# The product of theta and phi by seven products of 128 by 128

## The chip, the cores and the metric

The kernel runs on one core of a Trainium2 chip. The metric is the device time of one execution in microseconds (us); lower is better. All numbers are fp32.

## The reference

The input is `x`, 8 images of 512 channels and 32 by 32 positions (n = 1024). The first layer is an attention block with 8 heads and a residual. The second is a nonlocal block followed by a normalization over the batch. The change lies in the second layer:

```python
theta_x = _conv1x1(x, theta_w, theta_b).reshape(b, C_INTER, n)      # C_INTER = 256
phi_x = _conv1x1(x, phi_w, phi_b).reshape(b, C_INTER, n)
f_div_C = jnp.einsum('bcn,bdn->bcd', theta_x, phi_x) / n            # 256 by 256, a sum over 1024 positions
y = jnp.einsum('bcd,bdn->bcn', f_div_C, g_x).reshape(b, C_INTER, h, w)
z = _conv1x1(y, W_w, W_b) + x
```

## The kernel before, in words

The program is one straight line of instructions for 8 images, with buffers and waits set by a tile framework. The function `unshifted` does the work. A second function, `shifted`, is there for inputs whose scores would be too large, and is not entered in the runs shown.

For each image `b` the loop at L816 runs: attention (`attention`, scores at L462, weighted sums at L488); queries, values and keys of the next image (`heads_of`, `values`); the projection (`project`); theta and phi together (`theta_phi`, L610); and the nonlocal part (`nonlocal_`, L640).

Most large products are already made by the seven-product scheme, which replaces the eight products of a 2 by 2 block product by seven, with extra sums of blocks. `seven` (L263) writes the matmuls at L300, product after product (numbered 0 to 6). After each product it calls `read`, which adds the result into SBUF, and then a function given in `between` for that number. So `between` is how work of other kinds is put among the products.

Theta times phi is not made in that way. `make_f` (L630) makes it as 2 by 8 matmuls: for each half of theta's 256 columns, eight blocks of 128 positions are summed in PSUM, each by a 128 by 128 weight (theta) against 256 columns (theta's block of positions of `phi`). In this program's fp32, every matmul is recorded as two matmul records, each with a weight load of its own. The result `f`, 128 by 512 elements in one PSUM bank, goes to SBUF by one ScalarE instruction, which also applies the factor 1/n (L637). It is written into a spare part of the tile that holds the weights of `g`.

`nonlocal_` runs the seven products of `g` (called `pg`), and calls `make_f` after product 5 (L662). Then `f` and the weights `ww` give the folded weights `wf` (L670, two products of two matmuls, `pwf`; ScalarE copies them to SBUF at L671). From `wf` and `g` come the last seven products (`pz`), preceded by sums of `g` (L683, tiles `tg`) and sums of `wf` (L686, tile `ws`) on VectorE.

The tile `tp` holds theta in columns 0 to 255 and phi in columns 256 to 511, in eight blocks of 128 positions. It is complete in steps: theta's two halves after products 5 and 3 of `ptp`, phi's two halves after products 4 and 6.

What sets the order: instructions wrapped in `pe`, `dve` or `sp` stay in the written order on their engine; the framework places the others by its own estimates. Blocks such as `ww`, `wf` and the sums come from a ring of ten buffers (`block`, L76), handed out in turn: a new block waits until the buffer's last readers are done. Weights come by `load_w` (L124) from two buffers in turn, through the DMA queue of SyncE (SP); so a weight load waits until the product that used the buffer is over, and what is behind it in the queue waits too. `ww` is loaded through the same queue (L643).

Images 0 to 4 go through `pz` at once. Image 5 stops after `wf`, which is put aside with `g` for the end (`late`). Image 6's `f` is made inside the attention of image 7, and image 7 is the last.

Of the kernel before, what the change touches and what calls it, by code (L numbers as in the profile page):

```python
# [11 lines left out]
ALU = mybir.AluOpType  # L12
# [4 lines left out]
P = 128  # L17
# [13 lines left out]
def unshifted(ctx: ExitStack, tc: tile.TileContext, a: dict, out: bass.AP):  # L31
    nc = tc.nc
    B, C, H, W = a["x"].shape
    N = H * W
    CC = C // P
    NB = N // P
# [4 lines left out]
    CI = a["WgT"].shape[1]  # L41
    IC = CI // P
# [19 lines left out]
    def pe(ins):  # L62
        tc.keep_in_program_order(ins)

    dve = sp = pe
# [10 lines left out]
    def block(name):  # L76
        return ring.tile([P, 2, 512], F32, tag="e", name=name)
# [14 lines left out]
    theta, phi = (a[n].rearrange("(c p) f -> p c f", p=P) for n in ("WthetaT", "WphiT"))  # L92
# [10 lines left out]
    def weight_sums(w, a21, which=(3, 4, 5, 6), pin=lambda ins: None):  # L103
        for to, l, r, op in ((3, a21, w[:, 2], ALU.add), (4, w[:, 3], w[:, 0], ALU.subtract),
                             (5, w[:, 0], a21, ALU.subtract), (6, w[:, 1], w[:, 4], ALU.subtract)):
            if to in which:
                pin(nc.vector.tensor_tensor(w[:, to], l, r, op))
# [9 lines left out]
    rest = {}  # L117
# [24 lines left out]
    def weights(name, sums_done=False):  # L142

        n, w = loaded.pop(0)
        assert n == name
        if name not in kept:
            if not sums_done:
                weight_sums(w, corner[name])
            if name not in ("WqT", "WkT"):
                keep("plain" if name == "WpT" else name, w)  # L150
        return w

    def keep(name, w):
        kept[name] = dram.tile([P, 14 * w.shape[3]], F32, tag=f"kept_{name}", name=f"kept_{name}")
        nc.sync.dma_start(kept[name], w.rearrange("p i k f -> p (i k f)"))
# [172 lines left out]
    xt = xp.tile([P, CC, N], F32, tag="x", name="x_0")  # L328
    heads = const.tile([P, P], F32, tag="heads", name="heads")
    nc.vector.memset(heads, 0.0)  # L330
    _, w_first = weights_tile("WqT", C // 2)
    loaded.append((queue.pop(0), w_first))
    corner["WqT"] = block("a21_WqT")[:, :, :C // 2]
    for x_part, w_part in (((0, 1, 0), (w_first[:, 0], 0, 0, 0, 1)), ((1, 2, 0), (w_first[:, 0], 0, 0, 1, 2)),
                           ((2, 4, 0), (w_first[:, 1], 0, 1, 0, 2)), ((0, 1, 1), (w_first[:, 2], 1, 1, 0, 2)),
                           ((1, 2, 1), (corner["WqT"], 1, 0, 0, 2)), ((2, 4, 1), ())):
        c0, c1, h = x_part
        at = slice(h * 512, (h + 1) * 512)
        nc.sync.dma_start(xt[:, c0:c1, at], x_v[0, :, c0:c1, at])
        if w_part:  # L340
            to, m, k, c0, c1 = w_part
            nc.scalar.dma_start(to[:, c0:c1], quarter("WqT", m, k)[:, c0:c1])
    ps = next_bank("warm_ps")[:, 0, :]
# [263 lines left out]
              early=b == B - 1, inner="WpT" if 0 < b < B - 1 else None)  # L607


    def theta_phi(b, w, data, between):  # L610
        tp = mats.tile([P, NB, 2 * CI], F32, tag="o", name=f"tp_{b}")

        def at(q):
            return tp[:, (int(q[1]) - 1) * NB // 2:int(q[1]) * NB // 2, (int(q[0]) - 1) * CI:int(q[0]) * CI]

        def as_tp(ps):
            return ps.rearrange("p h (i f) -> p (h i) f", f=CI)

        def first(q, ps):
            ins = nc.vector.tensor_tensor(at(q), as_tp(ps), tpb[:, int(q[0]) - 1].to_broadcast([P, NB // 2, CI]),  # L620
                                          ALU.add)
            if q == "11":
                dve(ins)

        seven(f"ptp_{b}", w, data, True, first,
              lambda q, ps: nc.vector.tensor_tensor(at(q), at(q), as_tp(ps), ALU.add),
              {0: lambda: "t3" in data or more_sums(data, (3, 4), pin=dve), **between})
        return tp

    def make_f(b, tp, ps):  # L630
        f = rest["WgT"][:, :IC * CI].rearrange("p (c d) -> p c d", c=IC)
        ps = ps[:, 0, :].rearrange("p (c d) -> p c d", c=IC)
        for c in range(IC):
            for i in range(NB):
                pe(nc.tensor.matmul(ps[:, c, :], tp[:, i, c * P:(c + 1) * P], tp[:, i, CI:],  # L635
                                    start=(i == 0), stop=(i == NB - 1)))
        nc.scalar.mul(f, ps, 1.0 / N)  # L637
        return f

    def nonlocal_(b, xt, data, f, wg, before_wf, between=None):  # L640

        ww = block(f"ww_{b}")
        nc.sync.dma_start(ww, a["WwT"].rearrange("(c p) f -> p c f", p=P))  # L643
        g = [w3.tile([P, N], F32, tag="acc", name=f"g_{b}_{d}") for d in range(IC)]
        fs = [f]

        def f_meanwhile():
            fs[0] = f(next_bank(f"pf_{b}"))

        def part(q):  # L650
            return g[int(q[0]) - 1][:, cols(q)]

        def first(q, ps):
            d = int(q[0]) - 1
            if between and q == "21":
                nc.vector.tensor_scalar(part(q), ps[:, 0, :], gb[:, d:d + 1], 1.0, ALU.add, ALU.mult)
            else:
                nc.scalar.activation(part(q), ps[:, 0, :], AF.Identity, bias=gb[:, d:d + 1])  # L658

        seven(f"pg_{b}", wg, data, False, first,  # L660
              lambda q, ps: nc.vector.tensor_tensor(part(q), part(q), ps[:, 0, :], ALU.add),
              between or {5: f_meanwhile}, early=bool(between))  # L662
        f = fs[0]

        before_wf()
        wf = block(f"wf_{b}")
        for d in range(IC):
            ps = next_bank(f"pwf_{b}_{d}")[:, 0, :]
            for c in range(IC):
                pe(nc.tensor.matmul(ps, f[:, c, d * P:(d + 1) * P], ww[:, c, :], start=(c == 0), stop=(c == IC - 1)))  # L670
            nc.scalar.copy(wf[:, d, :], ps)  # L671
        if b >= B - LATE:
            late[b] = xt, g, wf
            return
        half = C // 2
        ws = block(f"ws_{b}")
        w = [wf[:, 0, :half], wf[:, 1, :half], wf[:, 1, half:]] + [ws[:, i, j * half:(j + 1) * half]
                                                                 for i in range(2) for j in range(2)]
        tg = block(f"tg0_{b}"), block(f"tg1_{b}")
        t = [tg[i // 2][:, i % 2, :] for i in range(4)]  # L680
        b11, b12, b21, b22 = (g[k][:, h * 512:(h + 1) * 512] for k in range(2) for h in range(NH))
        for to, l, r in ((t[0], b12, b11), (t[1], b22, t[0]), (t[2], b22, b12), (t[3], b21, t[1])):
            nc.vector.tensor_tensor(to, l, r, ALU.subtract)  # L683
        for to, l, r, op in ((3, wf[:, 0, half:], w[2], ALU.add), (4, w[3], w[0], ALU.subtract),
                             (5, w[0], wf[:, 0, half:], ALU.subtract), (6, w[1], w[4], ALU.subtract)):
            nc.vector.tensor_tensor(w[to], l, r, op)  # L686

        class Blocks:
            shape = (P, 7, 1, half)

            def __getitem__(self, at):
                _, i, k, m = at
                return w[i][:, m]

        def first_z(q, ps):
            for m in range(2):
                c = rows(q).start + m
                at = xt[:, c, cols(q)]
                nc.vector.scalar_tensor_tensor(at, ps[:, m, :], wb[:, c:c + 1], at, ALU.add, ALU.add)

        data = {"11": b11, "21": b21, "22": b22, "t1": t[0], "t2": t[1], "t3": t[2], "t4": t[3]}
        data = {n: d.rearrange("p (k n) -> p k n", k=1) for n, d in data.items()}
        seven(f"pz_{b}", Blocks(), data, False, first_z, add_to(xt))
        for oc in range(CC):
            for h in range(NH):
                nc.vector.bn_stats(stats[:, oc, b * NH + h, :], xt[:, oc, h * 512:(h + 1) * 512])
            nc.sync.dma_start(spill[b][:, oc, :], xt[:, oc, :])
# [83 lines left out]
    b11, b12, b21, b22 = quarters_of(xt)  # L791
    t = [block(f"t{i}_x_0") for i in range(4)]
# [7 lines left out]
    data = {"11": b11, "21": b21, "22": b22, "t1": t[0], "t2": t[1], "t3": t[2], "t4": t[3]}  # L800
# [15 lines left out]
    for b in range(B):  # L816
# [22 lines left out]
        between = None  # L839
        if not last:  # L840
# [25 lines left out]
            later_k = []  # L866
# [5 lines left out]
        else:  # L872
# [3 lines left out]
            between = {4: late_unit(b - 1, 0, sums_now=False)}  # L876
# [14 lines left out]
        data = data_sums(quarters_of(xt), f"x1_{b}", (1, 2, 3, 4) if last else (1, 2))  # L891
        if last:
            reload_chunks(B - LATE)
        elif b > B - LATE and b != B - 2:
            z[b] = [xt[:, cc, :] for cc in range(CC)]
        tp = theta_phi(b, weights("tp"), data, {} if last else
                       {1: lambda: [one() for one in later_k[:2]], 2: lambda: [one() for one in later_k[2:]],
                        4: lambda: bound_scores(b + 1, q, k, peak_q, peak_k)})
        load_w(nc.sync)

# [9 lines left out]
        if b == B - 2:  # L910
            held.update(x=xt, tp=tp)
        else:
            nonlocal_(b, xt, data, lambda ps: make_f(b, tp, ps), weights("WgT"), before_wf)
            load_w(nc.sync)
            if b in spill_g:
                put_away(b)
        xt = nxt.get("x")
# [6 lines left out]
    ps = next_bank("count")[:, 0, :]  # L924
# [214 lines left out]
```

## Time and profile before

| | |
|---|---|
| median of 4 runs | 2149.22 us (2148.83 to 2150.01) |
| the profiled execution, as timed | 2149.39 us |
| its span in the profile | 2147.6 us |
| TensorE matmuls (PE) | 2124.4 us busy |
| weight loads (PEld) | 1123.0 us busy, beside the matmuls |
| VectorE (DVE) | 1401.8 us busy |
| ScalarE (ACT) | 746.1 us busy |
| GpSimd (POOL) | 193.2 us busy |

The time of the execution is 1.8 us more than its span. PE and PEld are one engine with two rows: a weight load can run while an earlier matmul streams. A matmul's recorded length holds its latency, so that the pace of a row of matmuls is read from the distance of their starts. In a line of the timeline the first two numbers are the start and the length of a merged group in us, "x32" is its number of records, and the bracket is the engine's idle time before it and what ended that. `pf` is the PSUM tile of theta times phi, and `w_WgT` in `w_WgT<-pf` is the tile that holds `f`.

### The profile page before, as it was taken

What the parts mean: (1) busy time and instruction counts of PE and PEld (TensorE: products, weight loads), DVE (VectorE), ACT (ScalarE), POOL (GpSimd) and SP (SyncE); (2) the same over time, 40 slices, a digit from 0 to 9 for tenths busy, and PEclk for the clock granted to TensorE, in tenths of its full rate; (3) what the DMA queues carried; (4) which work ended last, traced back from release to release, by engine and by line L of the source; (5) the groups of instructions that cost most, each with busy time, mean ns of one, the idle gap of its engine ahead of it and who ended that gap; (6) DMA issues with size and microseconds to landing.
All of it is one profiled execution on the core that took longest, in us unless ns stands there. A gap on an engine that the chain in (4) does not pass through costs nothing.

```text
span 2147.6 us, 30080 instructions
## 1 busy us (share of the span) xinstructions
PE 2124.4 (99%) x12510; PEld 1123.0 (52%) x12510; DVE 1401.8 (65%) x1699; ACT 746.1 (35%) x854; POOL 193.2 (9%) x242
## 2 busy tenths in 40 slices
PE   9999999999999999999999999999999999999996
PEld 4534664356733567335663366633666347743462
DVE  6466666667576675766657667576674676757736
ACT  1464104641046310463105621056212652056106
POOL 0111000110001100011000100011000110001000
PEclk9999999999999999999999999999999999999998
DMA  6433443334143331433324343233434235122758
GB/s 241 137 46 62 135 163 126 50 72 127 73 130 48 80 116 72 133 50 81 110 98 113 48 100 98 98 107 50 107 139 151 40 48 139 52 60 38 225 200 340
DMA packets 53967, 231.02 MB, mean 108 GB/s; under 512 B 9792, under 2 KB 16192, under 8 KB 46272
## 3 DMA queue, kind: packets, MB, share of 16 engines
q1 hardware_dynamic: 42144, 199.26, 27.5%
q0 software_dynamic: 10192, 28.46, 11.0%
q8 instruction: 100, 1.64, 0.3%
q10 hardware_dynamic: 1488, 1.32, 0.2%
q14 instruction: 43, 0.35, 0.1%
HBM read 141.84 MB, written 46.27 MB: 88 GB/s over the span
## 4 chain that ended last, share of the span: by engine, by line
PE 97%; ACT 1%; DVE 1%; DMA 0%; issue 0%; SPq 0%; DVEq 0%; ACTq 0%
PE ps L462 21%; PE po L488 20%; PE pv L300 9%; PE ptp L300 9%; PE pp L300 7%; PE pq L300 6%; PE pk L300 6%; PE pg L300 4%; PE pk_in_s L255 3%; PE pq_in_s L255 3%; PE pf L635 3%; PE pz L300 2%; PE pp_in_s L255 2%; PE pwf L670 1%; ACT z L787 1%; PE pz L746 1%
## 5 line engine op out<-in xcount | busy, mean ns | idle before, releaser
L465 ACT ACTIVATE e<-ps 128x1024 f32<-128x1024 f32 x512 | 522.5, 1024 | 431.3 <-PE ps L462 425.8
L471 DVE TENSOR_TENSOR acc<-acc,e 128x1024 f32<-128x1024 f32 x384 | 469.9, 1224 | 143.6 <-ACT e L465 140.3
L462 PE MATMUL ps<-q,k 64*64 64x512 f32 x4096 | 529.4, 590 | 0.0
L488 PE MATMUL po<-e,v 64*64 64x512 f32 x4096 | 528.7, 589 | 0.0
L488 PEld LDWEIGHTS po<-e,v 64*64 64x64 f32 x4096 | 156.6, 133 | 282.8 <-issue 275.4
L462 PEld LDWEIGHTS ps<-q,k 64*64 64x64 f32 x4096 | 155.5, 133 | 283.8 <-issue 274.8
L501 POOL DMA_DIRECT2D fold<-acc x189 | 147.2, 779 | 982.3 <-DMA fold<-acc 573.7
L469 DVE TENSOR_TENSOR acc<-e,e 128x1024 f32<-128x1024 f32 x64 | 78.3, 1224 | 144.0 <-ACT e L465 144.0
L658 ACT ACTIVATE g<-pg,gb 128x512 f32<-128x512 f32 x31 | 21.3, 687 | 407.6 <-PE pg L300 407.5
L300 PE MATMUL pv<-w_WvT,t_x 128*128 128x256 f32 x512 | 116.4, 381 | 0.0
L300 PE MATMUL ptp<-w_tp,t_x 128*128 128x256 f32 x512 | 114.4, 379 | 0.0
L417 ACT COPY v<-pv 128x1024 f32<-128x1024 f32 x32 | 32.4, 1012 | 213.9 <-PE pv L300 213.9
L300 PEld LDWEIGHTS pv<-w_WvT,t_x 128*128 128x128 f32 x512 | 96.6, 190 | 18.5 <-issue 5.7
L300 PEld LDWEIGHTS ptp<-w_tp,t_x 128*128 128x128 f32 x512 | 97.3, 190 | 13.2
L300 PE MATMUL pp<-t_o,w_WpT 128*128 128x512 f32 x208 | 100.8, 592 | 0.0
L300 PE MATMUL pk<-t_x,w_WkT 128*128 128x512 f32 x200 | 100.0, 592 | 0.0
L300 PE MATMUL pq<-t_x,w_WqT 128*128 128x512 f32 x200 | 99.8, 592 | 0.0
L429 POOL TENSOR_SCALAR q<-q,gates 128x1024 f32<-128x1024 f32 x32 | 35.1, 1108 | 718.8 <-DVE gates L427 718.8
L300 PE MATMUL ptp<-w_tp,x 128*128 128x256 f32 x384 | 87.4, 381 | 0.0
L300 PE MATMUL pv<-w_WvT,x 128*128 128x256 f32 x384 | 86.8, 379 | 0.0
L324 DVE TENSOR_TENSOR q<-q,pq_in_s 128x256 f32<-128x256 f32 x119 | 48.5, 419 | 51.2 <-PE pq_in_s L255 38.5
L324 DVE TENSOR_TENSOR k<-k,pk_in_s 128x256 f32<-128x256 f32 x119 | 47.8, 418 | 50.0 <-PE pk_in_s L255 36.1
(178 smaller groups left out, 2297.6 us busy)
## 6 DMA issues: line engine op xcount, KB each, us to landing
fold<-acc POOLq DMA_DIRECT2D x189, 128.0 KB, 3.1
w_WqT<-kept_WqT SPq DMA_DIRECT2D x7, 2368.0 KB, 8.8
w_WkT<-kept_WkT SPq DMA_DIRECT2D x7, 2368.0 KB, 9.0
r<-den_d SPq DMA_DIRECT2D x32, 512.0 KB, 7.4
x<-in_x_dram SPq DMA_DIRECT2D x30, 512.0 KB, 5.7
w_WpT<-kept_WpT SPq DMA_DIRECT2D x6, 2176.0 KB, 8.4
w_WvT<-kept_WvT SPq DMA_DIRECT2D x7, 1792.0 KB, 7.1
w_tp<-kept_tp SPq DMA_DIRECT2D x7, 1792.0 KB, 7.2
```

Source lines behind the costliest of these rows:

```text
L255: pe(nc.tensor.matmul(ps, a[wi], d[di], start=s not in begun, stop=True, skip_group_check=True))
L300: pe(nc.tensor.matmul(to_ps, lhsT(k), rhs(k), start=(s, at) not in begun, stop=(k == nk - 1), skip_group_check=True))
L324: pin(nc.vector.tensor_tensor(at, at, ps if len(ps.shape) == 3 else ps.unsqueeze(1), ALU.add))
L417: seven(f"pv_{b}", w, data, True, lambda q, ps: nc.scalar.copy(at(q), as_v(ps)), lambda q, ps: dve(nc.vector.tensor_tensor(at(q), at(q), a ...
L429: nc.gpsimd.tensor_scalar(q[:, p, :], q[:, p, :], gate[:, p:p + 1], 1.0, ALU.mult, ALU.mult)
L462: pe(nc.tensor.matmul(ps[c * P // 2:(c + 1) * P // 2, j, :], k[r, p, keys], q[r, p, h * 512:(h + 1) * 512], start=True, stop=True, skip_gr ...
L465: nc.scalar.activation(e, ps, AF.Exp, scale=SCALE)
L469: nc.vector.tensor_tensor(accs[u], es[u, 0], e, ALU.add)
L471: ins = nc.vector.tensor_tensor(accs[u], accs[u], e, ALU.add)
L488: pe(nc.tensor.matmul(ps[j * D:(j + 1) * D, r, :], v[keys, m, (2 * p + j) * D:(2 * p + j + 1) * D], e[keys, j, :], start=(m == 0), stop=(m ...
L501: nc.gpsimd.dma_start(to, part_of, accum_op=ALU.add)
L635: pe(nc.tensor.matmul(ps[:, c, :], tp[:, i, c * P:(c + 1) * P], tp[:, i, CI:], start=(i == 0), stop=(i == NB - 1)))
```

## The change

For images 0 to 5, `f` is made by the seven-product scheme as well. Images 6 and 7 stay with `make_f`.

- `f_sums` (new) makes four sums of 128 by 512 elements of theta on VectorE, and later four of phi. The blocks are halves of the 256 columns and halves of the positions. Theta's sums are called after product 5 of `ptp`, phi's at the start of `nonlocal_`, ahead of the load of `ww`. They take four ring buffers.
- `seven_f` (new) makes seven products of four matmuls each, 128 by 128 weights against 128 columns. They go to seven regions of two PSUM banks. One copy and seven additions on VectorE then make the four blocks of `f`. One of theta's sums is overwritten with an intermediate sum.
- `f` is called after product 4 of `pg`, where it was called after product 5.
- The factor 1/n goes from the ScalarE instruction on `f` (which is gone in these images) to the ScalarE instruction that copies `wf`.

```diff
+    def f_sums(b, tp, k0):
+        name = f"{'phi' if k0 else 'theta'}_{b}"
+        both = block(f"s0_{name}"), block(f"s1_{name}")
+        t = [both[i // 2][:, i % 2, :].rearrange("p (i f) -> p i f", f=P) for i in range(4)]
+        c1, c2 = ([tp[:, h * NB // 2:(h + 1) * NB // 2, k0 + c * P:k0 + (c + 1) * P] for h in range(2)]
+                  for c in range(2))
+        if k0:
+            b11, b21, b12, b22 = *c1, *c2
+            ops = ((0, b12, b11, ALU.subtract), (1, b22, t[0], ALU.subtract), (2, b22, b12, ALU.subtract),
+                   (3, b21, t[1], ALU.subtract))
+        else:
+            b11, b12, b21, b22 = *c1, *c2
+            ops = ((0, b21, b22, ALU.add), (1, t[0], b11, ALU.subtract), (2, b11, b21, ALU.subtract),
+                   (3, b12, t[1], ALU.subtract))
+        for to, l, r, op in ops:
+            dve(nc.vector.tensor_tensor(t[to], l, r, op))
+        return {"11": b11, "12": b12, "21": b21, "22": b22, **{f"s{i + 1}": t[i] for i in range(4)}}
+
+    def seven_f(theta, phi, ps):
+        f = rest["WgT"][:, :IC * CI].rearrange("p (c d) -> p c d", c=IC)
+        at = [ps[:, i // 4, i % 4 * P:(i % 4 + 1) * P] for i in range(7)]
+        for to, l, r in zip(at, ("11", "s2", "12", "s3", "s1", "22", "s4"), ("11", "s2", "21", "s3", "s1", "s4", "22")):
+            for i in range(NB // 2):
+                pe(nc.tensor.matmul(to, theta[l][:, i, :], phi[r][:, i, :], start=(i == 0), stop=(i == NB // 2 - 1),
+                                    skip_group_check=True))
+        f11, f12, f21, f22 = (f[:, c, d * P:(d + 1) * P] for c in range(2) for d in range(2))
+        u = theta["s1"][:, 0, :]
+        dve(nc.vector.tensor_copy(f11, at[0]))
+        for to, l, r, op in ((u, f11, at[1], ALU.add), (f11, f11, at[2], ALU.add), (f22, u, at[3], ALU.add),
+                             (f12, u, at[4], ALU.add), (f21, f22, at[5], ALU.add), (f22, f22, at[4], ALU.add),
+                             (f12, f12, at[6], ALU.add)):
+            dve(nc.vector.tensor_tensor(to, l, r, op))
+        return f
...
+        if theta:
+            phi = f_sums(b, tp, CI)
+            f = lambda ps: seven_f(theta, phi, ps)
         ww = block(f"ww_{b}")
...
-              between or {5: f_meanwhile}, early=bool(between))
+              between or {4 if theta else 5: f_meanwhile}, early=bool(between))
...
-            nc.scalar.copy(wf[:, d, :], ps)
+            nc.scalar.mul(wf[:, d, :], ps, 1.0 if scaled else 1.0 / N)
...
+                       {5: lambda: b < B - 2 and of_theta.append(f_sums(b, tps[0], 0)), 1: lambda: [one() for one in later_k[:2]], 2: lambda: [one() for one in later_k[2:]],
```

More of the change, by code (lines that the diff above doesn't have):

```diff
@@ L607, in project @@
               early=b == B - 1, inner="WpT" if 0 < b < B - 1 else None)
+    tps = []
     def theta_phi(b, w, data, between):
         tp = mats.tile([P, NB, 2 * CI], F32, tag="o", name=f"tp_{b}")
+        tps[:] = [tp]
         def at(q):
@@ L638, in make_f, with nonlocal_ @@
         return f
-    def nonlocal_(b, xt, data, f, wg, before_wf, between=None):
+    def nonlocal_(b, xt, data, f, wg, before_wf, between=None, theta=None, tp=None):
+        scaled = theta is None
+        if theta:
+            phi = f_sums(b, tp, CI)
+            f = lambda ps: seven_f(theta, phi, ps)
         ww = block(f"ww_{b}")
@@ L895, in unshifted @@
             z[b] = [xt[:, cc, :] for cc in range(CC)]
+        of_theta = []
         tp = theta_phi(b, weights("tp"), data, {} if last else
-                       {1: lambda: [one() for one in later_k[:2]], 2: lambda: [one() for one in later_k[2:]],
+                       {5: lambda: b < B - 2 and of_theta.append(f_sums(b, tps[0], 0)), 1: lambda: [one() for one in later_k[:2]], 2: lambda: [one() for one in later_k[2:]],
                         4: lambda: bound_scores(b + 1, q, k, peak_q, peak_k)})
@@ L912, in unshifted @@
         else:
-            nonlocal_(b, xt, data, lambda ps: make_f(b, tp, ps), weights("WgT"), before_wf)
+            nonlocal_(b, xt, data, lambda ps: make_f(b, tp, ps), weights("WgT"), before_wf,
+                      theta=of_theta[0] if of_theta else None, tp=tp)
             load_w(nc.sync)
```

## The prediction

> **What bounds the kernel now.** I read the page's first part, then its chain of work that ended last, then the waits of TensorE. The first fence is part 1 of the page, the second the chain by engine, the third the longest waits of the matmuls (engine and line, what was waited for, total us, times, longest).
>
> ```profile
> PE 2124.4 (99%) x12510; PEld 1123.0 (52%) x12510; DVE 1401.8 (65%) x1699; ACT 746.1 (35%) x854; POOL 193.2 (9%) x242
> ```
>
> ```profile
> PE 97%; ACT 1%; DVE 1%; DMA 0%; issue 0%; SPq 0%; DVEq 0%; ACTq 0%
> ```
>
> ```profile
> PE warm_ps L345 <- DVE heads L330: 1.1, 1, 1.1
> PE den L434 <- PE pg L300: 0.6, 1, 0.6
> ```
>
> TensorE is the chain from end to end and waits for about 2 us in all. So a microsecond taken from its matmul stream comes off the time, as long as nothing else becomes late; VectorE and ScalarE work is free as long as it stays under a matmul. Next, the stage itself, in the timeline of image 2: first TensorE, then VectorE.
>
> ```profile
> 845.12 1.88 PE L300 MATMUL pg<-x,w_WgT 128*128 128x512 f32 x4
> 846.84 7.07 PE L635 MATMUL pf<-tp 128*128 128x256 f32 x32
> 853.75 1.88 PE L300 MATMUL pg<-t_x,w_WgT 128*128 128x512 f32 x4
> 855.47 3.60 PE L670 MATMUL pwf<-ww,w_WgT 128*128 128x512 f32 x8
> 858.90 1.88 PE L300 MATMUL pz<-g,wf 128*128 128x512 f32 x4
> ```
>
> ```profile
> 836.74 1.23 DVE L620 TENSOR_TENSOR tp<-ptp,tpb 128x1024 f32<-128x1024 f32 x1 [2.23 <-PE ptp L300]
> 843.66 0.69 DVE L661 TENSOR_TENSOR g<-g,pg 128x512 f32<-128x512 f32 x1 [5.70 <-PE pg L300]
> ...
> 848.37 0.68 DVE L683 TENSOR_TENSOR tg<-g,g 128x512 f32<-128x512 f32 x1
> 848.98 0.68 DVE L683 TENSOR_TENSOR tg<-g,tg 128x512 f32<-128x512 f32 x1
> 858.00 0.42 DVE L686 TENSOR_TENSOR ws<-wf 128x256 f32<-128x256 f32 x1 [8.34 <-ACT wf L671]
> ```
>
> Theta times phi holds TensorE from 846.84 to 853.75: 6.91 us for 32 records, 0.216 each. Records of 512 columns come at 0.429 (1.72 for four). Both are a little under 0.84 ns a column plus 2 ns: the columns set the pace, not the weight loads. VectorE has two holes in this stage, 5.70 and 8.34 us.
>
> How fast are records of 128 columns? No warm stream of them is in the trace. Two places bound it: the warm-up at the start, which is 16 such records at half the clock (first row), and four products of one column in image 0, where only weight loads of the same size follow each other (two rows, five loads apart).
>
> ```profile
> 1.13 3.49 PEld L345 LDWEIGHTS warm_ps<-heads 128*128 128x128 f32 x16 [1.13 <-DVE heads L330]
> ...
> 218.31 0.19 PEld L191 LDWEIGHTS den<-ones,fold 128*128 128x128 f32 x1
> ...
> 218.87 0.19 PEld L191 LDWEIGHTS den<-ones,fold 128*128 128x128 f32 x1
> ```
>
> Warm-up: the last of 16 loads (333 ns long) starts at 4.29, so one every 0.21 us; halved, about 0.107. That is the pace of the columns alone, with a load for each record beside them. One column: (218.87 - 218.31) / 5 = 0.112 us from load to load.
>
> **What the Trainium skill says.** "TensorE: Matmul & The Clock Gate", section "LDWEIGHTS (loading the stationary operand)", gives a load as its columns over 1.2, 107 ns for 128; the 0.112 above agrees. The same page, "Back-to-back issue gap", says that in streams of loads and matmuls the pace is set by both, with 81 ns for 128 columns where the matmul alone takes 56: 25 ns more than perfect overlap. The rows here show no such loss, but no warm stream of this size either. "PSUM — Partial Sum Buffer", "PSUM bank collisions raise a hardware error", says that engines are to be kept apart by bank, not by address. The order of instructions of the changed kernel agrees: of the eight VectorE instructions that read `pf`, only the first, the copy, waits for TensorE, so it waits for all seven products.
>
> **The change, part by part** (times of image 2; the six images repeat it to 0.01 us).
>
> *Matmuls.* Removed: 32 records, 6.91 us. Added: 7 products x 4 matmuls x 2 records = 56. Columns fall from 32 x 256 = 8192 to 56 x 128 = 7168, weight loads rise from 32 to 56. At the pace of the columns, 0.109 (half of 0.216 plus half of the fixed 2 ns), it is 6.10 us, a gain of 0.80; at the pace of the loads, 0.112, it is 6.27, a gain of 0.64; with the skill's 25 ns added, 0.134 to 0.137, it is 7.5 to 7.7, a loss of 0.6 to 0.8. The change gains as long as a record takes less than 6.91 / 56 = 0.123. I take 0.112: a load starts as the matmul before it starts, and the next matmul cannot start before that load is in, whatever its columns; and in the warm-up both lie fully beside each other. Six images: 6 x 0.64 = 3.8 us.
>
> *Theta's sums.* Four of 128x512 at 0.61 from start to start (the L683 rows: 848.37, 848.98) are 2.4 us. They follow the sum of product 5 (ends 834.5) and fill the 2.23 us hole before 836.74, so phi's last addition starts 0.3 late. Nothing on TensorE waits for it then.
>
> *Phi's sums.* Another 2.4 us, in the 5.70 us hole: from 838.2 to 840.7. The products now start at 845.12, since `pg` product 5 comes after them: 4.4 us to spare.
>
> *The sums of `f`.* They wait for the last product, at 845.12 + 6.27 = 851.39, and start at 851.6. A 128x128 VectorE operation has 0.28 to 0.29 us (L169) and comes each 0.3 us or so. Copy and five sums give f11 and f21 at 853.4. The addition of `pg` product 5 is next on VectorE (it can't run before 853.3), then two sums: done at 854.6. TensorE meanwhile has two products of `pg`, 3.43 us, and reaches `pwf` at 854.8, where f11 and f21 are wanted first; f12 and f22 are wanted at 856.5. To spare: 1.4 and 1.9 us. If the cover were gone, each us of lateness would cost six. Queued behind this wait on VectorE is only the sum of `pg` product 5, then the three `tg` sums, 854.6 to 856.4. Before, they were done at 849.7; they now have 0.9 us until the first `ws` sum, which comes when `wf` does, as before.
>
> *ScalarE.* One 0.60 us instruction less for each image, and the copy of `wf` becomes a multiplication of the same size (0.59 and 0.60): nothing on the path, since between `f` and `pwf` it had 1.7 us of `pg` as cover already.
>
> *DMA order.* On the SP queue `ww` stood ahead of the next `w_WqT`; in the changed kernel it stands behind it, so it is held by that load's wait for the end of `ptp`. The rows are the SP timeline, then the page's median us to landing.
>
> ```profile
> 812.75 0.39 SPq L643 DMA_DIRECT2D ww<-in_WwT_dram  x1
> 836.74 0.33 SPq L134 DMA_DIRECT2D w_WqT<-kept_WqT  x1
> ...
> w_WqT<-kept_WqT SPq DMA_DIRECT2D x7, 2368.0 KB, 8.8
> ...
> ww<-in_WwT_dram SPq DMA_DIRECT2D x8, 512.0 KB, 5.5
> ```
>
> `ww` goes out at 837.1 instead of 812.75. Behind the whole of `w_WqT` and with a fifth more of its time it lands near 836.7 + 8.8 + 2 = 847.5; `pwf` wants it at 854.8. Hidden, with 7 us to spare; uncovered, it would hold TensorE by what is missing. `w_WqT` itself is wanted an attention later. In image 5 the reloads of `x` and the putting aside of `g` change places behind `ww`; both lie in front of an attention of some 110 us (871 to 981). The four ring buffers fall to blocks whose readers are done: the sums take those of the projection's sums, over by 812.
>
> Sum: -3.8 us on TensorE, nothing elsewhere. From the profiled execution's 2149.39 it gives 2145.6; the median shown is 0.17 lower, so 2145.4.
>
> **The rivals.**
>
> *The pace of the columns.* If loads hide wholly, 0.109 a record: 6 x 0.80 = 4.8 us, 2144.4. The warm-up speaks for it; the 0.112 from load to load speaks against.
>
> *Loads and matmuls get in each other's way when warm.* Place: the 56 records of `pf`. At 0.137 each, 7.67 us, 0.76 more than now in each image: +4.6 us, 2153.8, slower. It decides from 0.123 on. For it: the skill's sustained figure, and that loads and columns here need nearly the same time, so that neither has slack. Against: the warm-up, where they also need the same, at exactly the pace of the columns.
>
> *`f` or `ww` comes late at `pwf`.* It takes VectorE steps over 0.5 us (six steps from 851.6 to 854.8), or `ww` over 17 us to land, to begin; 0.64 us of lateness an image eats the gain, and the time stays at 2149.2. Against: the margins above.
>
> **How the numbers follow.** Chances: likeliest case (0.112, all hidden) 0.62; pace of the columns 0.14; loads and matmuls in each other's way 0.15; late `f` or `ww` 0.09. The bound of 0.2% is 4.3 us, about what a measurement of this kernel can tell from no change; the likeliest case, -3.8, lies just inside, and with half a us from the runs and 1 ns on the pace (0.3 us) I give a fifth of it, 0.13, to over 4.3. Faster: 0.13 + 0.14 = 0.27. Slower: 0.13 of the third case and 0.03 of the last = 0.16. Within: 0.57. The range goes from 2143.8 (the column pace, and half a us) to 2150.5 (a pace of 0.127, or a late `f`); past it lie most of the third case and little else.
>
> **What would show it.** Right: the `pf` group is 56 records over about 6.27 us from its first start to the next `pg`, in all six images; no idle time on TensorE before `pwf` and `pz`; the VectorE copy starts after the last product; `ww` issued just after `w_WqT`. Wrong: starts over 0.123 apart, a wait of `pwf` for VectorE or for a DMA, or a wait of the second `pz` product for `ws`.

## The result, and the profile after

| | median, us | runs |
|---|---|---|
| before | 2149.57 (2148.83 to 2153.03) | 52 |
| after | 2145.8 (2144.84 to 2147.97) | 32 |

The ratio of after to before is 0.9982, with a 95% interval of 0.9978 to 0.9987: faster by 0.18%, or 3.8 us. The forecast was 2145.4 us, and a gain of 3.8. That the two agree to a tenth is in part luck: single runs of one kernel lie up to 4.2 us apart, and the stages themselves gained 3.9 us, as shown below.

The span fell from 2147.6 to 2143.4 us. First the three views that said what bounds the kernel, for the kernel after: busy time by engine, the chain by engine, the longest waits of the matmuls.

```profile
PE 2119.6 (99%) x12654; PEld 1123.7 (52%) x12654; DVE 1447.7 (68%) x1795; ACT 743.0 (35%) x848; POOL 193.2 (9%) x242
```

```profile
PE 97%; ACT 1%; DVE 1%; DMA 1%; issue 0%; ACTq 0%
```

```profile
PE warm_ps L345 <- DVE heads L330: 1.1, 1, 1.1
PE pq L300 <- DVE t_x L842: 0.7, 1, 0.7
PE den L434 <- PE pg L300: 0.5, 1, 0.5
```

TensorE is still the chain. VectorE works 46 us more and none of it shows in the waits. There are 144 more matmul records (6 x 24), and yet TensorE is busy for 4.8 us less. The wait of `pq` lies in the start-up of image 0, where the first loads come in.

The stage of image 2 again, TensorE in the timeline after:

```profile
842.12 1.88 PE L300 MATMUL pg<-t_x,w_WgT 128*128 128x512 f32 x4
843.84 1.05 PE L658 MATMUL pf<-tp 128*128 128x128 f32 x8
844.73 1.06 PE L658 MATMUL pf<-s_phi,s_theta 128*128 128x128 f32 x8
845.62 1.06 PE L658 MATMUL pf<-tp 128*128 128x128 f32 x8
846.52 1.95 PE L658 MATMUL pf<-s_phi,s_theta 128*128 128x128 f32 x16
848.30 1.06 PE L658 MATMUL pf<-s_phi,tp 128*128 128x128 f32 x8
849.20 1.06 PE L658 MATMUL pf<-tp,s_theta 128*128 128x128 f32 x8
850.09 1.88 PE L300 MATMUL pg<-x,w_WgT 128*128 128x512 f32 x4
851.81 1.88 PE L300 MATMUL pg<-t_x,w_WgT 128*128 128x512 f32 x4
853.52 3.60 PE L713 MATMUL pwf<-ww,w_WgT 128*128 128x512 f32 x8
```

The group of `pf` goes from 843.84 to 850.09: 6.25 us for 56 records, 0.1116 each, where it was 6.91 for 32; the other five images have the same two lengths to 0.01 us. No bracket with an idle time stands ahead of `pwf` at 853.52. VectorE in the same stage:

```profile
832.00 1.22 DVE L629 TENSOR_TENSOR tp<-tp,ptp 128x1024 f32<-128x1024 f32 x1 [2.38 <-PE ptp L300]
833.26 1.51 DVE L649 TENSOR_TENSOR s_theta<-tp 128x512 f32<-128x512 f32 x1
834.80 0.69 DVE L649 TENSOR_TENSOR s_theta<-s_theta,tp 128x512 f32<-128x512 f32 x1
...
836.61 1.22 DVE L623 TENSOR_TENSOR tp<-ptp,tpb 128x1024 f32<-128x1024 f32 x1
...
850.29 0.29 DVE L662 COPY w_WgT<-pf 128x128 f32<-128x128 f32 x1 [5.56 <-PE pf L658]
850.62 0.29 DVE L666 TENSOR_TENSOR s_theta<-w_WgT,pf 128x128 f32<-128x128 f32 x1
850.94 0.29 DVE L666 TENSOR_TENSOR w_WgT<-w_WgT,pf 128x128 f32<-128x128 f32 x1
851.14 0.48 DVE L666 TENSOR_TENSOR w_WgT<-s_theta,pf 128x128 f32<-128x128 f32 x2
851.54 0.28 DVE L666 TENSOR_TENSOR w_WgT<-w_WgT,pf 128x128 f32<-128x128 f32 x1
852.01 0.69 DVE L704 TENSOR_TENSOR g<-g,pg 128x512 f32<-128x512 f32 x1 [0.19 <-PE pg L300]
```

The copy starts 0.20 us after TensorE has gone on from the last product to `pg` at 850.09, so VectorE did wait for all seven. The copy reads only the first of the two banks, and that one was full after four products; whether it could start then, 2.7 us earlier, no run tries. f11 is in SBUF at 851.23 and f21 at 851.82; `pwf` begins at 853.52. The first sum of theta took 1.51 us and not 0.69, which the prediction did not have; the run `theta_later` below takes that up.

Where in the program the time went is seen from one small product, `bound`, which runs once for each image. Its first and last start enclose all six changed stages. The lines give records, lengths in ns, then the two starts; before, then after:

```profile
L425 PE MATMUL bound<-peak_q,heads x16: 169/210/253, 67.7 to 1871.5; 128*128 128x4 f32 x16
```

```profile
L425 PE MATMUL bound<-peak_q,heads x16: 169/210/253, 67.7 to 1867.6; 128*128 128x4 f32 x16
```

From 1803.8 to 1799.9: 3.9 us, and 6 x (6.907 - 6.251) is 3.9. The other 0.3 us of the two spans lie outside the six stages. Outside them two things differ from execution to execution in all the traces below: the first loads (the first `bound` starts between 67.7 and 69.1), and the last image's reload of its softmax denominators (TensorE stood for it between 0 and 2.2 us). What is left outside differs by some tenths. So in what follows a kernel's effect is read between its first and last `bound`, and the times of single runs are taken with a grain of salt.

### The profile page after: what moved, and what is told of

The parts are those of the page before. It is cut to its first block, busy times and chain, and to the rows that moved or that the text cites. A ratio compares the mean times of both kernels' runs of the same rounds, so it can differ in the third digit from the quotient of the medians.

```text
span 2143.4 us, 30444 instructions
## 1 busy us (share of the span) xinstructions
PE 2119.6 (99%) x12654; PEld 1123.7 (52%) x12654; DVE 1447.7 (68%) x1795; ACT 743.0 (35%) x848; POOL 193.2 (9%) x242
## 4 chain that ended last, share of the span: by engine, by line
PE 97%; ACT 1%; DVE 1%; DMA 1%; issue 0%; ACTq 0%
PE ps L462 21%; PE po L488 21%; PE pv L300 9%; PE ptp L300 9%; PE pp L300 7%; PE pk L300 6%; PE pq L300 5%; PE pg L300 5%; PE pk_in_s L255 3%; PE pq_in_s L255 3%; PE pz L300 2%; PE pf L658 2%; PE pp_in_s L255 2%; PE pwf L713 1%; ACT z L830 1%; PE pz L789 1%
```

## The experiments

Ratios are to the kernel before, on the same chip; "between the bounds" is the distance just explained (before 1803.8, after 1799.9).

### columns_96: what sets the pace of 0.1116

```diff
-                pe(nc.tensor.matmul(to, theta[l][:, i, :], phi[r][:, i, :], ...
+                n = P if i == 0 else 96
+                pe(nc.tensor.matmul(to[:, :n], theta[l][:, i, :], phi[r][:, i, :n], ...
```

> The changed kernel, with columns 96 to 127 left out in three of the four matmuls of each of the seven products. If the weight loads set the pace (my theory), the pf group keeps its 56 records at 0.112 us, 6.25 us from its first start to the next pg, and the time stays near 2145.8. If the columns set it, the 42 narrow records come at 0.082 (96 x 0.84 ns + 2 ns): 14 x 0.112 + 42 x 0.082 = 5.0 us, and the time is 7.5 us lower.

One run, 2146.69 us. The timeline of its `pf`, image 2, first row, last row and what follows:

```profile
844.73 1.03 PE L659 MATMUL pf<-tp 128*128 128x128 f32 x8
...
850.06 1.06 PE L659 MATMUL pf<-tp,s_theta 128*128 128x128 f32 x8
850.95 1.48 PE L300 MATMUL pg<-x,w_WgT 128*128 128x512 f32 x3
```

The group takes 6.22 us, with a quarter of the columns gone from three matmuls in four. (A merged row prints the shape of its first record.) Between the bounds 1799.9, the same as the changed kernel's. The columns do not set the pace at 128 columns; something that the full and the narrow records have in common does: the load of 128 weight columns, or a fixed time.

### columns_96_weights_64: the load, or a fixed time for issuing

```diff
-                pe(nc.tensor.matmul(to, theta[l][:, i, :], phi[r][:, i, :], ...
+                n, m = (P, P) if i == 0 else (96, 64)
+                pe(nc.tensor.matmul(to[:m, :n], theta[l][:, i, :m], phi[r][:, i, :n], ...
```

> As columns_96, and the same three of four matmuls load only 64 of the 128 weight columns, so half of the output partitions are left out of them too. If the time of a load goes with its columns, a load of 64 is over in half of 0.107 and the 96 columns set the pace: 0.082 for the narrow records, 5.0 us for the group, about 7.5 us less in all than the changed kernel. If 0.112 is a fixed time for issuing a load and a matmul, nothing changes: 6.25 us.

One run, 2152.83 us: 1806.7 between the bounds, 6.8 more than the changed kernel, where 7.5 less was expected. The forecast of the total missed, yet the question asked is answered inside the group. Two loads of 64 columns in a run of six narrow records, three loads apart, each from a short stretch of the timeline:

```profile
846.75 0.14 PEld L659 LDWEIGHTS pf<-tp 128*64 128x64 f32 x1
...
846.99 0.14 PEld L659 LDWEIGHTS pf<-tp 128*64 128x64 f32 x1
```

(846.99 - 846.75) / 3 = 0.08: the pace of 96 columns, as forecast. So 0.1116 is not a fixed time for issuing a load and a matmul; with half the weight columns it is gone, while the moving columns are as in `columns_96`. Together the two runs leave the load of 128 weight columns. What was not forecast lies between the narrow and the full records:

```profile
846.30 1.02 PE L659 MATMUL pf<-tp 128*128 128x128 f32 x8
847.25 1.13 PE L659 MATMUL pf<-s_phi,s_theta 128*128 128x128 f32 x8
848.31 0.38 PE L659 MATMUL pf<-tp 128*128 128x128 f32 x1
```

A product of two full and six narrow records comes each 1.05 us (847.25 and 848.31 apart by 1.06, 846.30 and 847.25 by 0.95, where the first had its load done ahead). By the two paces it would be 2 x 0.112 + 6 x 0.082 = 0.72. Each product has two changes between weights of 128 and of 64 columns, and some 0.3 us goes with them. The change from 128 to 96 moving columns is not the cause, since `columns_96` has it too, at no cost; the number of weight columns and that of output partitions change together, and no run separates them. The whole group takes 7.30 us.

### eight_128: the narrower matmul without the seven products

The kernel before, with `make_f` cut by columns as well:

```diff
-        for c in range(IC):
+        parts = [(c, slice(d * P, (d + 1) * P)) for c in range(IC) for d in range(2)] if b < B - 2 else [...]
+        for c, d in parts:
             for i in range(NB):
-                pe(nc.tensor.matmul(ps[:, c, :], tp[:, i, c * P:(c + 1) * P], tp[:, i, CI:], ...
+                pe(nc.tensor.matmul(ps[:, c, d], tp[:, i, c * P:(c + 1) * P], tp[:, i, CI + d.start:CI + d.stop], ...
```

> The kernel before, with theta times phi of images 0 to 5 cut into eight products' worth of 128 by 128 matmuls (64 records, no sums), all else as before. It prices the narrower matmul alone. At 0.1116 us a record: 64 x 0.1116 = 7.14 us for 6.91, +0.24 an image, +1.4 us in all over the kernel before (2151.0). If columns of 128 cost no more than half of 256, 0.109: 6.98, +0.4 us.

Ratio 1.0011 (1.0002 to 1.0019); the median is 2.0 us above before. Its `pf` in the timeline, and what follows:

```profile
847.82 7.31 PE L637 MATMUL pf<-tp 128*128 128x128 f32 x64
854.96 1.45 PE L300 MATMUL pg<-t_x,w_WgT 128*128 128x512 f32 x3
```

7.14 us for 64 records, 0.1116 each, and between the bounds 1805.2, 1.4 more than before: as forecast, to a tenth. This splits the gain of the change for each image: cutting the columns in two costs 0.24 us, leaving out one product of eight saves 0.89, together the 0.66.

### f_after_5: whether the earlier place is needed

```diff
-              between or {4 if theta else 5: f_meanwhile}, early=bool(between))
+              between or {5: f_meanwhile}, early=bool(between))
```

> The changed kernel with f made after product 5 of pg again, so one product of pg (1.72 us) instead of two lies between f's products and pwf. From the changed kernel's trace f11 is in SBUF 1.14 us after the last product and f21 1.73 us after; the loads of pwf that want them come 1.29 and 2.15 us after. My theory: no wait, the same time as the changed kernel, ratio to before 0.998. Rival: the second product of pg is needed as cover, pwf waits for VectorE by 0.2 to 0.6 us an image, 1 to 4 us in all, ratio 0.9987 to 1.000.

Ratio 0.9985 (0.9978 to 0.9992). TensorE in image 2, the last of `pf` and what follows, with no idle time:

```profile
852.30 1.06 PE L658 MATMUL pf<-tp,s_theta 128*128 128x128 f32 x8
853.20 1.88 PE L300 MATMUL pg<-t_x,w_WgT 128*128 128x512 f32 x4
854.91 3.60 PE L713 MATMUL pwf<-ww,w_WgT 128*128 128x512 f32 x8
```

Between the bounds 1799.9 (69.1 to 1869.0): the same as the changed kernel. Its median is half a microsecond higher, with the intervals overlapping; in its profile the first `bound` is 1.4 us late. One product of `pg` is cover enough.

### f_after_6: no cover

```diff
-              between or {4 if theta else 5: f_meanwhile}, early=bool(between))
+              between or {6 if theta else 5: f_meanwhile}, early=bool(between))
```

> The changed kernel with f made after product 6 of pg, so nothing lies between f's products and pwf. My theory: the load of f11 waits for VectorE until about 1.2 us after the last product, and TensorE stands for 1.2 to 1.5 us an image: 7 to 9 us in all, time near 2154, slower than before. Rival (the sums of f cost nothing wherever they lie): as the changed kernel, 2145.8.

2154.2 us, ratio 1.002 (1.0013 to 1.0027): slower than before. Image 2 in the timeline, TensorE's matmuls and then its weight loads:

```profile
855.36 1.06 PE L658 MATMUL pf<-tp,s_theta 128*128 128x128 f32 x8
857.45 3.70 PE L713 MATMUL pwf<-ww,w_WgT 128*128 128x512 f32 x8 [1.03 <-DVE w_WgT L666]
```

```profile
857.44 0.30 PEld L713 LDWEIGHTS pwf<-ww,w_WgT 128*128 128x128 f32 x2 [1.22 <-DVE w_WgT L666]
858.04 0.19 PEld L713 LDWEIGHTS pwf<-ww,w_WgT 128*128 128x128 f32 x1 [0.29 <-DVE w_WgT L666]
```

The first load of `pwf` waits for f11, and a later one 0.29 us more. Between the bounds it is 1807.7, so 7.8 us more than the changed kernel, 1.3 for each image: the VectorE sums of `f` cost 1.3 us when they are uncovered, twice the 0.66 us that the products gain.

### sums_only: VectorE's sums of theta and phi alone

```diff
-        scaled = theta is None
+        scaled = True
         if theta:
             phi = f_sums(b, tp, CI)
-            f = lambda ps: seven_f(theta, phi, ps)
...
-              between or {4 if theta else 5: f_meanwhile}, early=bool(between))
+              between or {5: f_meanwhile}, early=bool(between))
```

so that the factor 1/n stays on `f`.

> The changed kernel's eight sums of theta and phi are made (with their four ring buffers, and with ww behind the next weights in the queue), but f is made by 16 matmuls of 256 columns after product 5 of pg as before, and 1/n stays with f. My theory: these sums are wholly hidden, so the time is that of the kernel before within 0.4 us, with the pf group at 6.91 us. Rival: VectorE's sums, the buffers or the place of ww cost something of themselves: over 1 us more than before.

Ratio 1.0004 (0.9996 to 1.0012): the interval holds no difference, but the median is 1.0 us up, over the 0.4 us that was expected and at the mark of the rival. The profile says where its own execution lost 2.1 us of span:

```profile
L425 PE MATMUL bound<-peak_q,heads x16: 169/210/253, 67.7 to 1871.5; 128*128 128x4 f32 x16
```

```profile
PE pp L300 <- DVE o L571: 2.2, 1, 2.2
```

Between the bounds it is 1803.8, the kernel before to the tenth, with 48 sums more. The 2.2 us are one wait, for the last image's denominators, where no sum was added; the same wait was 0.2 before, 1.6 in `f_after_6`, and none in the kernel after. In the six stages the sums, their buffers and the later place of `ww` cost nothing. The thirteen runs lie between 2149.88 and 2152.12 us, a spread of the size of that wait. Whether this kernel meets the wait more often than the kernel before, or by chance, is not shown: there is one profile of each.

### ww_ahead: the place of ww in the queue

```diff
+        ww = block(f"ww_{b}")
+        nc.sync.dma_start(ww, a["WwT"].rearrange("(c p) f -> p c f", p=P))
         if theta:
             phi = f_sums(b, tp, CI)
             f = lambda ps: seven_f(theta, phi, ps)
-        ww = block(f"ww_{b}")
-        nc.sync.dma_start(ww, a["WwT"].rearrange("(c p) f -> p c f", p=P))
```

> The changed kernel with ww asked for ahead of phi's sums, as before. If the place of ww in the queue is hidden (my theory), ww lands over 20 us earlier in its stage and the time stays at the changed kernel's, 2145.8 within 0.6. If it holds pwf unseen, the time falls.

2146.01 us, ratio 0.9982 (0.9974 to 0.999), between the bounds 1799.9. The SP queue of the kernel after, then of this one:

```profile
835.45 0.32 SPq L134 DMA_DIRECT2D w_WqT<-kept_WqT  x1
835.87 0.38 SPq L686 DMA_DIRECT2D ww<-in_WwT_dram  x1
```

```profile
811.72 0.39 SPq L683 DMA_DIRECT2D ww<-in_WwT_dram  x1
835.70 0.33 SPq L134 DMA_DIRECT2D w_WqT<-kept_WqT  x1
```

It goes out 24 us earlier, and nothing is gained. In the kernel after, `ww` takes 9.8 us to land (the page's median) instead of 5.5, so it is there at about 845.7; it is wanted at 853.5.

### theta_later: the first sum of theta

```diff
-                       {5: lambda: b < B - 2 and of_theta.append(f_sums(b, tps[0], 0)), 1: ...
+                       {1: ...
...
+            if b < B - 2:
+                of_theta.append(f_sums(b, tp, 0))
             nonlocal_(...
```

> The changed kernel with theta's four sums after the last product of theta and phi, beside phi's, instead of after product 5. In the changed kernel's trace the first sum of theta takes 1.51 us instead of 0.69, in all six images, and ends 0.55 us after GpSimd's last gate multiplication. If GpSimd's work causes it, the first sum takes 0.69 here, where GpSimd is idle; if it is the first read of theta or the wait ahead of it, it stays 1.5. The time stays at the changed kernel's: the eight sums end about 842, before pf's start.

One run, 2145.35 us; between the bounds 1799.8 from the rounded starts, the changed kernel's within 0.1. The sums of theta (the first and third of each image in one row, lengths in ns as least, median, most), in the kernel after and in this one, and GpSimd in the kernel after:

```profile
L649 DVE TENSOR_TENSOR s_theta<-tp x12: 681/1094/1522, 307.3 to 1624.3; 128x512 f32<-128x512 f32 x12
```

```profile
L649 DVE TENSOR_TENSOR s_theta<-tp x12: 680/682/685, 310.6 to 1626.8; 128x512 f32<-128x512 f32 x12
```

```profile
829.83 4.39 POOL L429 TENSOR_SCALAR q<-q,gates 128x1024 f32<-128x1024 f32 x4 [93.13 <-DVE gates L427]
```

GpSimd multiplies by the gates until 834.22. The sum that starts at 833.26 ends 0.55 us after that, and away from it no sum takes over 0.69. The two other causes named beforehand, the first read of theta and the wait ahead of it, would have kept it at 1.5. VectorE's addition just before, at 832.00, ran beside the same multiplication and took its usual 1.22 us; one of its two operands lies in PSUM.

### image_7_too: one image more

The experiments leave one place where the same gain can be had cheaply: image 7, whose `f` has two products after it as cover.

```diff
+        late_sums = theta and b == B - 1
...
+              between or ({4: phi_and_ww, 5: f_meanwhile} if late_sums else {4 if theta else 5: f_meanwhile})
...
-        tp = theta_phi(b, weights("tp"), data, {} if last else
+        tp = theta_phi(b, weights("tp"), data, {5: lambda: of_theta.append(f_sums(b, tps[0], 0))} if last else
```

`phi_and_ww` makes phi's sums and loads `ww`.

> The changed kernel with f of image 7, the last, made by seven products too. Theta's sums come after product 5 of its theta and phi, phi's sums and the load of ww after product 4 of pg (the ring's buffers are taken until then), f after product 5; product 6 and a late product of z (5.1 us) lie between f and pwf. My theory: its pf group falls from 6.91 to 6.25 us with no new wait, 0.66 us off the changed kernel, near 2145.1, ratio to before 0.998. Rival: ww, asked for near 2071 instead of 2044 and 5 to 11 us on the way, or phi's sums, come late and give the 0.66 back or more.

2145.44 us, ratio 0.998 (0.9972 to 0.9988). The end of its last `pf` and what follows:

```profile
2074.31 1.05 PE L658 MATMUL pf<-tp 128*128 128x128 f32 x8
...
2080.56 1.88 PE L300 MATMUL pg<-t_x,w_WgT 128*128 128x512 f32 x4
2082.28 3.60 PE L797 MATMUL pz<-gwf 128*128 128x512 f32 x8
2085.71 3.60 PE L721 MATMUL pwf<-ww,w_WgT 128*128 128x512 f32 x8
```

The group takes 6.25 us for 6.91 with no wait behind it. In the time this is not shown: 2145.44 and 2145.8 were not measured side by side, and the intervals overlap. Nor do the two profiles show it beyond the group: from the last `bound` to the end of the span each takes 275.8 us (1868.6 to 2144.4, and 1867.6 to 2143.4). In this one TensorE stood 0.4 us for the last image's denominators, and in the kernel after it did not. It is a version as good as the changed one; that it is 0.66 us better remains an expectation.

## Why the prediction was right, point by point

- *Matmuls.* The sum was 56 records at 0.112, 0.64 us an image; measured 0.1116 and 0.656. The reason given, that the loads set the pace, stands: fewer moving columns change nothing (`columns_96`), fewer weight columns do (`columns_96_weights_64`), and `eight_128` has the same 0.1116 without the seven products. The rival of 0.109 would have been the pace of the columns, and `columns_96` speaks against it. The rival of 0.137, loads and matmuls in each other's way, did not happen; what the Trainium skill's "TensorE: Matmul & The Clock Gate" ("Back-to-back issue gap") gives for 128 columns, 25 ns more than the matmul alone, is here 2 to 3 ns over the estimated 0.109. The section names no number format for its sizes, and here the measurement decides. The warm-up was the weaker of the two bounds: by the figures shown with it, (4.29 - 1.13) / 15 / 2 is 0.105, and 0.107 without its first step, both under the 0.1116 measured. That it ran at half speed shows, in the trace of the kernel before, in the loads of `pq` behind it: those at 5.56 and 6.42 are 0.86 us apart, those at 7.09 and 7.52 are 0.43. The rows of one column, 0.112, gave the right pace.
- *Theta's sums.* They were expected to hold phi's last addition back by 0.3 us. That began at 836.61, 1.4 after its product ended at 835.25, where 0.2 is usual: 1.2 late. The missing term is above all the 0.8 us beside GpSimd; another 0.1 is that the second sum reads the first and so comes later than 0.61 (phi's two are 0.73 apart). "SBUF — State Buffer", section "Who interferes with whom", of the Trainium skill states the first: a VectorE instruction with two SBUF inputs contends with a GpSimd instruction that reads SBUF. The trace agrees, with 1.51 for 0.69. It cost no time, since `pf` starts 3.4 us after phi's sums (4.4 was forecast).
- *The sums of f.* Expected: f11 and f21 at 2.0 us after the last product, all at 3.2. Measured: 1.73 and 3.0 (852.61 + 0.48 = 853.09). The step was taken as 0.3 us throughout; it is about 0.32 for the first two, where an operation reads what the one before wrote or overwrites what it read, and 0.20 for the next three. The margin was right in kind but counted too small: 1.4 us to spare would not cover the loss of one product of `pg` (1.72 us), yet `f_after_5` waits for nothing, because f11 alone is wanted first and f21 only 0.86 us later.
- *ScalarE and the factor 1/n.* As said: the scaled copy of `wf` takes 0.60 us for 0.59 and is not on the path.
- *The DMA order.* `ww` was expected at 847.5 with 7 us to spare, and lands at about 845.7 with 7.8 (the stage itself lies 1.3 us earlier by then). `ww_ahead` shows that its place costs nothing.
- *Late f or ww.* Neither occurred. The place where a late `f` decides is now known: behind product 6, at 1.3 us an image.
- *What a measurement can tell.* The prediction took 0.2% as about the least. The interval, 0.13% to 0.22% faster, is narrower: it keeps this gain apart from no change, but not from 0.2%.

## What to carry to other kernels

When a product is cut into smaller blocks to save one of eight, price it by the pace of the smaller matmul and not by the columns: here 128 columns cost 0.1116 us a record against 0.108 for half of 256, so that 7/8 of the work takes 0.905 of the time. The sums that come with it were free here only while other matmuls covered them; the chain from the last product to the first load that reads the result (here 1.3 us) had to lie beside TensorE work. And where a gain is 0.2% and the start-up varies by more than a microsecond, the distance between two fixed instructions in the trace shows to a tenth what the medians leave open.

## What the runs showed that was not expected

- Where weight loads of 128 and of 64 columns alternated, some 0.3 us went with each change there and back, as much as four narrow records; within a run of one width the loads stayed hidden.
- A VectorE sum of two SBUF operands took 1.51 us instead of 0.69 while GpSimd was at its multiplication, in six images of six, and 0.68 when it was moved away from it.
- Most of what differs between the traces outside the changed stages sits in two places: the first loads (up to 1.4 us) and one wait of the last image for a transfer (0 to 2.2 us).
